# Involution network on one core: the end of the last image, with means taken two rows at a time, a transform over pairs of rows, sums on ScalarE and stores on SyncE

## The chip, the cores and the metric

The kernel runs on one NeuronCore of a Trainium2 chip. The metric is the device time of one execution in microseconds (us); a time without a profile is the median of several executions. Engines are named as in the profile: PE is TensorE (matmul), PEld its weight loads, DVE is VectorE, ACT is ScalarE, POOL is GpSimd and SP is SyncE, which here only issues DMAs. Everything is float32. An fp32 matmul shows in the profile as two passes, each with its own weight load and its own MATMUL record, so "x112" on a matmul line is 56 matmuls.

## The reference

The input is 4 images of 256 channels, 56 x 56. Four residual layers follow one another: `x = x + L(gn(x))` with a group norm over 32 groups of 8 channels ahead of each. Layers 0 and 2 are involutions (a 7 x 7 filter made per pixel and group from the image itself), layer 1 is a pair of 3 x 3 convolutions. Layer 3, whose end is changed here, is a pair of gates:

```python
def _L3_conv_ref(x, W, b):
    cf = jnp.fft.fft2(x, axes=(-2, -1)).real.mean(axis=(-2, -1))
    cf = jax.nn.sigmoid(cf @ W.T + b)
    x_cft = x * cf[:, :, None, None]
    sf = jnp.fft.fft2(x.mean(axis=1, keepdims=True), axes=(-2, -1)).real.mean(axis=1)
    x_sft = x * sf[:, None, :, :]
    return x_cft + x_sft
...
x = x + _L3_conv_ref(_gn(x), L3_conv_W, L3_conv_b)
```

The mean of the real part of a transform is its first pixel, so the channel gate `cf` needs only the normed value at pixel (0, 0) of every channel. The pixel gate `sf` is the real part of the 2-D transform of the mean over channels of the normed image. The output is `x + xn * (cf + sf)` with `xn = gn(x)`.

## The kernel before

The channels are two blocks `cb` of 128, one per set of partitions. Layers 0 and 2 share `involution_layer`. A unit is one image and one block; the last of the eight is image 3, block 1. In a unit, `tap_matrices` (L460) makes the filter matrices in 32 steps, with hooks: small pieces of other work, generators stepped by `place`, are put behind step n. DVE adds the bias in three steps of four (L489) and ACT in the fourth (L482). Then `apply` (L501) runs over seven columns `tx` of 8 pixels: PE multiplies (L513), ACT and DVE combine the four or two groups (L528, L533) and DVE adds into the image block `xs` (L540). `next_windows` (L371) transposes the strip of a later column on PE and has SP copy it about with four DMAs (L388, L390). `column_sums` (L924) takes the statistics of a finished column on DVE, one column late. Everything between `since` and `in_order` is pinned: each engine runs its instructions in the order in which the code emits them, and SP and POOL issue their DMAs in that order too.

The gates of images 0 to 2 are computed while later units run: `gate_chunk` (L668) works on POOL, which also issues their loads and stores. For image 3, block 0's channel mean goes through `channel_mean` (L568) as a hook, and block 1 comes after the last `apply`, in this order:

- `last_sums` takes the statistics of the last column; `last_normed(b, 0)` (L701) makes `xn` of block 0 on ACT (L715).
- `last_mean` (L724): the channel mean of block 1 before the group norm is known. One matmul for each column x of the image, with the 56 pixels of the column as weights (a stride of 56 elements) and the 16 group sums as the moving operand (L735), gives 56 rows x 56 columns x 16 groups in two PSUM banks.
- `norm_steps` (L190): statistics, two matmuls with `gavg` (L197, L208), DVE steps between them, and `rsqrt` with its power on POOL (L139).
- The mean goes on: L738 and L741 spread scale and shift, DVE multiplies 56 x 896 values (L747), sums over groups (L754) and adds (L757).
- `gate_factors` (L611): the channel gate (L623 on PE, a sigmoid on ACT at L630) and the first half of the transform over both blocks (L639, L649).
- `last_gates` (L760): the second half (L772), a product that lays eight rows side by side (L774), and then seven chunks `j` of 8 rows. In each, PE spreads `sf` over the partitions (L783), DVE forms `(sf + f) * xn` for each block (L787), block 0 is summed and stored by POOL (L789, L790), block 1 is finished by ACT, which has the original `x` folded in by a scale and a shift (L792), and stored by SP (L793).

`dead` gives space in a block that is no longer used, `one_bank` and `two_banks` give the next of four double PSUM banks. After the last instruction every engine drains and meets the others at a barrier (L1558 in the profile).

Of the kernel before, what the change touches and what calls it, by code (L numbers as in the profile page):

```python
# [10 lines left out]
F32 = mybir.dt.float32  # L11
AF = mybir.ActivationFunctionType
ALU = mybir.AluOpType
# [3 lines left out]
P = 128  # L17
B, C, H, W = 4, 256, 56, 56
NB = C // P
# [3 lines left out]
R = 64  # L23
# [3 lines left out]
CR = 8  # L27
# [9 lines left out]
NTY, NTX = -(-H // TY), W // TX  # L37
# [34 lines left out]
def net_kernel(  # L72
# [169 lines left out]
    def involution_layer(layer, xin, xout, red, span, sb, xs_of, ahead=None, pending=None):  # L242

        with ExitStack() as es:
# [315 lines left out]
            def dead(b, cb, at, n):  # L560

                if b < B - 1:
                    return xs_of[b, cb][:, at : at + n]
                if None not in xs_of:
                    xs_of[None] = new_block()
                return xs_of[None][:, at : at + n]
# [125 lines left out]
            last_xn = {}  # L692
# [8 lines left out]
            def last_normed(b, cb):  # L701
# [11 lines left out]
                for j, xn in enumerate(pieces):  # L713
# [7 lines left out]
                    )  # L721
                    yield

            def last_mean(b, bank):  # L724


                cb, ng = NB - 1, P // 8
                xs = xs_of[b, cb].rearrange("p (h w) -> p w h", w=W)
                rstd, shift = (t[:, cb : cb + 1] for t in norms[3][b])
                by = gavg_sb.rearrange("p (g i) -> p i g", i=8)[:, 0, :]  # L730
                m = W // 2
                pair = two_banks()
                means = pair[:H, :, : m * ng].rearrange("y i (x g) -> y i x g", g=ng)
                for x in range(W):
                    nc.tensor.matmul(means[:, x // m, x % m, :], xs[:, x, :], by, start=True, stop=True)  # L735
                yield

                nc.tensor.matmul(bank[:H, 1 : 1 + ng], rstd.to_broadcast([P, H]), by, start=True, stop=True)  # L738
                scales = dead(b, cb, 4 * CR * W + NB * C, 32)[:H]
                yield  # L740
                nc.tensor.matmul(  # L741
                    bank[:H, 1 + ng : 2 + ng], shift.to_broadcast([P, H]), cmean[:, 0:1], start=True, stop=True
                )
                nc.vector.tensor_scalar(first_of[b][:, cb : cb + 1], xs[:, 0, 0:1], rstd, shift, ALU.mult, ALU.add)
                nc.vector.tensor_scalar_mul(scales[:, :ng], bank[:H, 1 : 1 + ng], 8.0 / C)
                parts = dead(b, cb, 2 * CR * W, 2 * CR * W)[:H].rearrange("y (i x g) -> y i x g", i=2, g=ng)
                nc.vector.tensor_tensor(  # L747
                    parts,
                    means,
                    scales[:, :ng].unsqueeze(1).unsqueeze(1).to_broadcast([H, 2, m, ng]),  # L750
                    ALU.mult,
                )
                nc.vector.tensor_copy(scales[:, ng : ng + 1], bank[:H, 1 + ng : 2 + ng])
                nc.vector.tensor_reduce(  # L754
                    m2_of[cb].rearrange("y (i x) -> y i x", i=2), parts, mybir.AxisListType.X, ALU.add
                )
                nc.vector.tensor_scalar_add(m2_of[cb], m2_of[cb], scales[:, ng : ng + 1])  # L757
                yield

            def last_gates(b):  # L760
                rstd, shift = norms[3][b]

                inv = small.tile([P, 1], F32, name="inv", bufs=1)
                nc.vector.reciprocal(inv, rstd[:, 1:2])
                cfx = small.tile([P, 1], F32, name="cfx", bufs=1)
                nc.vector.tensor_add(cfx, cf_of[b][:, 1:2], inv)
                back = small.tile([P, 1], F32, name="back", bufs=1)
                nc.vector.scalar_tensor_tensor(back, shift[:, 1:2], -1.0, inv, ALU.mult, ALU.mult)


                ps = one_bank()
                nc.tensor.matmul(ps[:H, :W], half, cs2_sb, start=True, stop=True)  # L772
                rows = dead(b, NB - 1, 0, CR * W)[:H]
                nc.vector.tensor_tensor(  # L774
                    rows.rearrange("y (r w) -> y r w", r=CR),
                    ps[:H, :W].unsqueeze(1).to_broadcast([H, CR, W]),
                    last_xn[0][:H].unsqueeze(2).to_broadcast([H, CR, W]),
                    ALU.mult,
                )
                for j in range(NCHUNK):  # L780
                    at = slice(j * CR * W, (j + 1) * CR * W)
                    sf = one_bank()[:, : CR * W]
                    nc.tensor.matmul(sf, last_xn[1][:H, j : j + 1].to_broadcast([H, P]), rows, start=True, stop=True)  # L783
                    for cb in range(NB):
                        xs, xn = xs_of[b, cb][:, at], last_xn[j, cb]
                        f = cfx if cb == 1 else cf_of[b][:, cb : cb + 1]
                        nc.vector.scalar_tensor_tensor(xn, sf, f, xn, ALU.add, ALU.mult)  # L787
                        if cb == 0:
                            nc.gpsimd.tensor_tensor(xs, xs, xn, ALU.add)  # L789
                            nc.gpsimd.dma_start(ov[b, cb][:, at], xs)  # L790
                        else:
                            nc.scalar.activation(xs, xn, AF.Identity, bias=back)  # L792
                            nc.sync.dma_start(ov[b, cb][:, at], xs)  # L793


            def step(g):
# [2 lines left out]
            def place(hooks, g, at):  # L799

                for n in at:
                    hooks.setdefault(n, []).append(step(g))
# [57 lines left out]
            for u, (b, cb) in enumerate(units):  # L860
                hooks = hooks0 if u == 0 else {}
                if prev is not None:
                    pb, pc, st, last_sums = prev
                    hooks.setdefault(1, []).append(last_column(last_sums))
                    place(hooks, norm_of(layer + 1, pb, pc, st), (2, 6, 7, 11, 12, 13))
                    if layer == 2 and u < 3:
                        g = norm_of(2, B - 1, u - 1, pending[1][u - 1])
                        place(hooks, g, (19, 20, 22, 23, 25, 26))
                    if layer == 2:
                        place(hooks, channel_mean(pb, pc), (13, 17))  # L870
                        if pc == 1:
                            place(hooks, gate_factors(pb), (17, 24, 27, 28, 30, 31))
                        elif pb == B - 1:
                            factors = gate_factors(pb)
                            place(hooks, factors, (20,))
                            hooks.setdefault(22, []).append(last_ones)
                    if layer == 2 and cb == 1 and b > 0:
                        for n in (16, 22, 28):
                            hooks.setdefault(n, []).extend((next_gate, next_load))
# [44 lines left out]
                def column_sums(tx, st=st, img=img):  # L924
                    nc.vector.bn_stats(st[:, tx, :], img[:, :, tx * TX : (tx + 1) * TX])  # L925
# [2 lines left out]
                    late[0].append(ahead)  # L928

                for tx in range(NTX):  # L930
                    for f in early[tx]:
                        f()
                    apply(b, cb, kt, tx, xws[u * NTX + tx])
                    next_windows()
                    next_strip()
                    if tx > 0:
                        column_sums(tx - 1)
                    for f in late[tx]:
                        f()
# [7 lines left out]
            if layer == 2:  # L947
                run(last_normed(b, 0))
                bank = one_bank()
                mean, norm = last_mean(b, bank), norm_steps(st, lambda: bank, 3, b, cb)  # L950
                next(mean)
                for _ in range(5):
                    next(norm)
                next(mean)
                next(norm)
                next(mean)
                normed = last_normed(b, cb)
                for _ in range(2):
                    next(normed)
                next(factors)  # L960
                run(normed)
                for _ in range(2):
                    next(factors)
                last_gates(b)
            in_order(since)

# [595 lines left out]
```

## Time and profile before

| | us |
|---|---|
| median of three executions | 1864.59 (1862.81 to 1867.78) |
| the profiled execution, its own time | 1861.41 |
| its span, first to last instruction | 1859.5 |
| PE busy | 1705.2 (92%) |
| DVE busy | 1430.2 (77%) |
| ACT busy | 751.4 (40%) |
| POOL busy | 432.0 (23%) |
| from the last matmul of `apply` (1814.7) to the end | 44.8 |

The profiled execution is one of the faster ones, 3.2 us under the median. Times inside it are counted from its first instruction. "Busy" is the union of an engine's records; "mean ns" is the length of one record, which for matmuls overlaps its neighbours. PEclk is the clock that was granted to PE as a share of the full one. A note in brackets says how long the engine had been idle ahead of a line and what released it.

### The profile page before, as it was taken

The page shows a single profiled execution, that of the slowest core. Times are in us where ns is not written, and L with a number is a line of the kernel's source. Part 1 is how long each engine was busy: PE and PEld are TensorE (multiplying, and loading weights), DVE is VectorE, ACT ScalarE, POOL GpSimd, SP SyncE. Part 2 cuts the span into 40 slices and gives each one's busy share as a digit, 9 for nine tenths or more (in the row PEclk, how much of TensorE's full clock was granted, in tenths as well). Part 3 has the DMA queues.
Part 4 walks back from the last instruction along what each step waited for, and adds up shares of the span by engine and source line. Part 5 has one row for each costly group of instructions (what it writes and reads, how often), then busy time and mean ns, then how long its engine had stood idle before and what let it go on. Part 6 is the DMA issues. An engine that isn't in the chain of part 4 may idle for free.

```text
span 1859.5 us, 55572 instructions
## 1 busy us (share of the span) xinstructions
PE 1705.2 (92%) x24028; PEld 1501.5 (81%) x24028; DVE 1430.2 (77%) x2824; ACT 751.4 (40%) x1662; POOL 432.0 (23%) x615
## 2 busy tenths in 40 slices
PE   5999999999859999999999999997989899898886
PEld 3888888888748988898899889985877887877874
DVE  5687778776668988998889888874777778778764
ACT  2445445454413222231232312113656556565543
POOL 2323433244210000000000000000000663672683
PEclk9999999999969999999999999998999999999985
DMA  3445544453543111120121111132433765763652
GB/s 100 150 147 178 154 121 138 156 154 106 159 129 101 41 62 61 61 68 25 61 71 58 51 48 33 54 122 63 154 129 127 207 209 174 201 213 118 196 164 75
DMA packets 65504, 215.67 MB, mean 116 GB/s; under 512 B 13487, under 2 KB 20444, under 8 KB 61420
## 3 DMA queue, kind: packets, MB, share of 16 engines
q1 hardware_dynamic: 44364, 141.60, 24.6%
q0 software_dynamic: 14848, 65.85, 10.9%
q10 hardware_dynamic: 6048, 4.68, 0.8%
q8 instruction: 189, 3.10, 0.7%
q14 instruction: 55, 0.45, 0.1%
HBM read 76.23 MB, written 49.15 MB: 67 GB/s over the span
## 4 chain that ended last, share of the span: by engine, by line
PE 67%; DVE 20%; DMA 4%; issue 3%; POOL 3%; ACT 2%; SPq 0%; DVEq 0%; POOLq 0%; ACTq 0%
PE mm L1336 20%; PE ps L513 15%; DVE kt L489 11%; PE mm L1254 10%; PE ps L471 8%; PE mm L1225 6%; PE ps L381 4%; DMA xw<-xw 2%; PE ps L433 2%; DVE un L533 2%; ACT hp L452 1%; DMA gx<-x 1%; PE ps L783 1%; DVE st L925 1%; DMA xs<-in_x_dram 1%
## 5 line engine op out<-in xcount | busy, mean ns | idle before, releaser
L513 PE MATMUL ps<-kt,xw 126*32 126x48 f32 (+1 forms) x12544 | 385.2, 236 | 57.0 <-DMA xw<-xw 19.2
L513 PEld LDWEIGHTS ps<-kt,xw 126*32 126x32 f32 (+1 forms) x12544 | 345.9, 122 | 102.6 <-issue 47.8
L471 PE MATMUL ps<-hp,z_sb 64*126 64x133 f32 x6144 | 387.2, 281 | 15.6 <-DVE kt L489 5.3
L471 PEld LDWEIGHTS ps<-hp,z_sb 64*126 64x126 f32 x6144 | 369.1, 188 | 30.4 <-DVE kt L489 6.6
L489 DVE TENSOR_TENSOR kt<-ps,zb_sb 126x798 f32<-126x798 f32 x384 | 357.8, 978 | 42.9 <-PE ps L471 42.4
L1336 PE MATMUL mm<-v,u_sb 128*128 128x280 f32 (+1 forms) x1728 | 383.2, 383 | 3.3 <-DVE v L1161 3.3
L1336 PEld LDWEIGHTS mm<-v,u_sb 128*128 128x128 f32 x1728 | 326.2, 189 | 57.4 <-DVE v L1161 3.6
L482 ACT ACTIVATE kt<-ps,zb_sb 126x133 f32<-126x133 f32 x768 | 224.0, 441 | 173.8 <-PE ps L471 173.8
L1254 PE MATMUL mm<-v,u_sb 128*128 128x252 f32 (+1 forms) x936 | 211.9, 387 | 12.6 <-DVE v L1145 12.6
L1254 PEld LDWEIGHTS mm<-v,u_sb 128*128 128x128 f32 x936 | 177.7, 191 | 43.1 <-issue 12.6
L533 DVE SCALAR_TENSOR_TENSOR un<-ps,par_sb,un 128x240 f32<-128x240 f32 x224 | 98.2, 456 | 101.9 <-ACT un L526 97.8
L533 DVE SCALAR_TENSOR_TENSOR un<-ps,s,un 128x240 f32<-128x240 f32 x224 | 102.4, 457 | 91.0 <-ACT un L528 86.7
L1373 POOL DMA_DIRECT2D x<-xs x24 | 13.1, 546 | 683.9 <-DVE xs L1372 538.6
L1321 ACT ACTIVATE res<-xs,shift,norm_sb 128x1120 f32<-128x1120 f32 (+1 forms) x24 | 30.2, 1259 | 234.8 <-DVE xs L1372 107.3
L538 POOL TENSOR_TENSOR xs<-un,xs 128x240 f32<-128x240 f32 x112 | 72.3, 665 | 223.0 <-DVE un L533 223.0
L382 ACT COPY xw<-ps 126x896 f32<-126x896 f32 x112 | 101.6, 907 | 50.1 <-PE ps L381 43.3
L381 PE MATMUL ps<-ident_sb,strip_sb 128*126 128x128 f32 x784 | 112.3, 284 | 1.4 <-DVE kt L489 0.8
L526 ACT ACTIVATE un<-ps,par_sb 128x240 f32<-128x240 f32 x112 | 50.1, 448 | 137.5 <-PE ps L513 134.9
L528 ACT ACTIVATE un<-ps,bn_t,s 128x240 f32<-128x240 f32 x112 | 60.1, 538 | 100.8 <-PE ps L513 94.6
L139 POOL TENSOR_TENSOR norm_sb<-norm_sb,mhalf 128x1 f32<-128x1 f32 x32 | 19.2, 602 | 351.0 <-DVE norm_sb L138 350.9
L1225 PE MATMUL mm<-xs,u_sb 128*128 128x126 f32 (+1 forms) x792 | 98.3, 277 | 1.3 <-DVE xs L1188 1.0
L1225 PEld LDWEIGHTS mm<-xs,u_sb 128*128 128x128 f32 x792 | 94.3, 191 | 2.7 <-issue 1.4
(224 smaller groups left out, 1962.3 us busy)
## 6 DMA issues: line engine op xcount, KB each, us to landing
xw<-xw SPq DMA_DIRECT2D x168, 252.0 KB
xw<-xw SPq DMA_DIRECT2D x224, 126.0 KB
xw<-xw POOLq DMA_DIRECT2D x56, 252.0 KB, 4.5
xs<-x SPq DMA_DIRECT2D x24, 560.0 KB
x<-xs POOLq DMA_DIRECT2D x8, 1568.0 KB, 8.1
xs<-x SPq DMA_DIRECT2D x8, 1568.0 KB
xs<-in_x_dram SPq DMA_DIRECT2D x6, 1568.0 KB
x<-xs SPq DMA_DIRECT2D x6, 1568.0 KB
```

What stands on the lines that cost most here:

```text
L381: nc.tensor.transpose(ps[:Q, k * P : (k + 1) * P], flat[:, k * Q : (k + 1) * Q], ident_sb)
L382: nc.scalar.copy(xw[:, :NSB, :], ps[:Q, : NSB * P].rearrange("q (n c) -> q n c", n=NSB))
L471: nc.tensor.matmul(ps[:Q, i, k * NT : (k + 1) * NT], z_sb[i * R : (i + 1) * R, cb * GB // 2 + gp, z0 : z0 + Q], hp[i * R : (i + 1) * R, py ...
L482: nc.scalar.activation(kt[:, g0 + i, pb, :, k], ps[:Q, i, k * NT : (k + 1) * NT], AF.Identity, bias=zb_sb[:, cb * GB + g0 + i, p0 + k : p0 ...
L489: nc.vector.tensor_tensor(kt[:, g0 : g0 + 2, pb], ps[:Q, :, : PB * NT].rearrange("q i (k t) -> q i t k", k=PB), zb_sb[:, cb * GB + g0 : cb ...
L513: nc.tensor.matmul(v[m * j : m * j + m, i, :, k * TP : (k + 1) * TP], xw[:, window(ty), m * j : m * j + m], kt[:, ng * j : ng * j + ng, :, ...
L528: nc.scalar.activation(part, o[0], AF.Identity, bias=bn["t4"][:, cb : cb + 1], scale=bn["s4"][ng][:, 0, cb : cb + 1])
L533: nc.vector.scalar_tensor_tensor(part, o[e], s, part, ALU.mult, ALU.add)
L538: nc.gpsimd.tensor_tensor(dst, u, dst, ALU.add)
L1225: nc.tensor.matmul(ps[:, co * m : (co + 1) * m], u[ci][:, co * P : (co + 1) * P], v2[:, e, : n // 2, ci * WT : (ci + 1) * WT], start=(ci = ...
L1254: nc.tensor.matmul(ps, u1_sb[:, ci, dy, k, co * P : (co + 1) * P], v[:, k, dy * NB + ci : (dy + n - 1) * NB + ci + 1 : NB, :], start=(j == 0),
L1336: nc.tensor.matmul(ps, u2_sb[:, ci, dy, k, co * P : (co + 1) * P], v[:, k, dy * NB + ci : (dy + n - 1) * NB + ci + 1 : NB, :], start=(j == 0),
```

## The change

The change touches only image 3 of layer 2's run.

- `last_dft` (new), a hook at step 21 of the last unit's `tap_matrices`: POOL clears a 128 x 224 table `along`; SP fills it with four DMAs and a second table `down` with one.
- `first_half` (new), hooks 28 and 29: block 0's half of the transform's first stage, two matmuls and two DVE copies, is done there.
- In the last column of the last unit, `column_sums` of the column before is emitted ahead of `apply` and not behind it.
- `last_mean`: 28 matmuls, each with two whole rows (112 pixels, next to one another) as weights, into one bank, and each a step of the generator. Sixteen 128 x 128 matmuls on the identity (`warm(16)`) come ahead of them, and the norm's steps are emitted between them. The products are 112 x 448 and the sums 112 x 28.
- `last_gates`: the transform of block 1 over pairs of rows: one matmul with `along` (224 columns), a DVE copy, then four matmuls with `down`, which are summed in PSUM with the matmul of block 0's half.
- Both blocks' outputs are finished by ACT as a scale and a shift, and all fourteen stores are issued by SP. POOL has no part in `last_gates`.

```diff
+            def last_dft(b):
+                n = 3 * CR * W
+                along = dead(b, NB - 1, n, 4 * W).rearrange("p (e c k) -> p e c k", e=2, c=2)
+                nc.gpsimd.memset(along, 0.0)
+                for e in range(2):
+                    for c in range(2):
+                        nc.sync.dma_start(along[e * W : (e + 1) * W, e, c], cs2[c * R : c * R + W])
+                down = dead(b, NB - 1, n + 4 * W, 4 * H).rearrange("p (e c k) -> p e c k", e=2, c=2)
+                nc.sync.dma_start(
+                    down[: H // 2], cs.rearrange("(y e) (c k) -> y e c k", e=2, c=2)
+                )
+                last_xn["dft"] = along, down
+            def first_half(b):
+                ps = one_bank()
+                for i in range(2):
+                    at = slice(i * R, i * R + W)
+                    nc.tensor.matmul(ps[at, :H], m2_of[0], sin_sb if i else cs2_sb[:H], start=True, stop=True)
+                yield
+                for i in range(2):
+                    at = slice(i * R, i * R + W)
+                    nc.vector.tensor_copy(half[at], ps[at, :H])
+                yield
...
-                for x in range(W):
-                    nc.tensor.matmul(means[:, x // m, x % m, :], xs[:, x, :], by, start=True, stop=True)
-                yield
+                for k in range(H // 2):
+                    nc.tensor.matmul(means[:, k, :], xs[:, k * n : (k + 1) * n], by, start=True, stop=True)
+                    yield
...
             def last_gates(b):
+                along, down = last_xn["dft"]
+                rows = dead(b, NB - 1, 0, CR * W)
+                ps = one_bank()
+                nc.tensor.matmul(
+                    ps[: H // 2, : 4 * W],
+                    last_xn["mean"],
+                    along[: 2 * W].rearrange("p e c k -> p (e c k)"),
+                    start=True,
+                    stop=True,
                 )
+                part = rows[: H // 2, : 4 * W].rearrange("p (e c k) -> p e c k", e=2, c=2)
+                nc.vector.tensor_copy(rows[: H // 2, : 4 * W], ps[: H // 2, : 4 * W])
+                ps = one_bank()
+                nc.tensor.matmul(ps[:H, :W], half, cs2_sb, start=True, stop=False)
+                for i in range(4):
+                    e, c = divmod(i, 2)
+                    nc.tensor.matmul(
+                        ps[:H, :W], down[: H // 2, e, c], part[:, e, c], start=False, stop=(i == 3)
+                    )
...
-                        f = cfx if cb == 1 else cf_of[b][:, cb : cb + 1]
-                        nc.vector.scalar_tensor_tensor(xn, sf, f, xn, ALU.add, ALU.mult)
-                        if cb == 0:
-                            nc.gpsimd.tensor_tensor(xs, xs, xn, ALU.add)
-                            nc.gpsimd.dma_start(ov[b, cb][:, at], xs)
-                        else:
-                            nc.scalar.activation(xs, xn, AF.Identity, bias=back)
-                            nc.sync.dma_start(ov[b, cb][:, at], xs)
+                        nc.vector.scalar_tensor_tensor(xn, sf, cfx[:, cb : cb + 1], xn, ALU.add, ALU.mult)
+                        nc.scalar.activation(xs, xn, AF.Identity, bias=back[:, cb : cb + 1])
+                        nc.sync.dma_start(ov[b, cb][:, at], xs)
...
+                            hooks.setdefault(21, []).append(lambda pb=pb: last_dft(pb))
                             hooks.setdefault(22, []).append(last_ones)
+                            place(hooks, first_half(pb), (28, 29))
...
+                    if layer == 2 and u == len(units) - 1 and tx == NTX - 1:
+                        column_sums(tx - 1)
...
-                    if tx > 0:
+                    if tx > 0 and not (layer == 2 and u == len(units) - 1 and tx == NTX - 1):
                         column_sums(tx - 1)
...
-                next(mean)
-                for _ in range(5):
-                    next(norm)
+                warm(16)
+                for _ in range(2):
+                    for _ in range(7):
+                        next(mean)
+                    for _ in range(2):
+                        next(norm)
+                for _ in range(H // 2 - 14):
+                    next(mean)
+                next(norm)
                 next(mean)
                 next(norm)
                 next(mean)
...
-                for _ in range(2):
-                    next(factors)
                 last_gates(b)
```

More of the change, by code (lines that the diff above doesn't have):

```diff
@@ L724, in last_mean @@
+            def first_half(b):
[8 more added lines that the diff above has]
+                yield
             def last_mean(b, bank):
-                cb, ng = NB - 1, P // 8
@@ L728, in last_mean @@
-                xs = xs_of[b, cb].rearrange("p (h w) -> p w h", w=W)
+                cb, ng, n = NB - 1, P // 8, 2 * W
+                xs = xs_of[b, cb]
                 rstd, shift = (t[:, cb : cb + 1] for t in norms[3][b])
                 by = gavg_sb.rearrange("p (g i) -> p i g", i=8)[:, 0, :]
-                m = W // 2
-                pair = two_banks()
-                means = pair[:H, :, : m * ng].rearrange("y i (x g) -> y i x g", g=ng)
-                for x in range(W):
-                    nc.tensor.matmul(means[:, x // m, x % m, :], xs[:, x, :], by, start=True, stop=True)
@@ L736, in last_mean @@
-                yield
-                nc.tensor.matmul(bank[:H, 1 : 1 + ng], rstd.to_broadcast([P, H]), by, start=True, stop=True)
-                scales = dead(b, cb, 4 * CR * W + NB * C, 32)[:H]
+                ps = one_bank()
+                means = ps[:n, : H // 2 * ng].rearrange("p (k g) -> p k g", g=ng)
+                for k in range(H // 2):
+                    nc.tensor.matmul(means[:, k, :], xs[:, k * n : (k + 1) * n], by, start=True, stop=True)
+                    yield
+                nc.tensor.matmul(bank[:n, 1 : 1 + ng], rstd.to_broadcast([P, n]), by, start=True, stop=True)
@@ L740, in last_mean @@
+                scales = dead(b, cb, 4 * CR * W + NB * C, 64)[:n]
                 yield
                 nc.tensor.matmul(
-                    bank[:H, 1 + ng : 2 + ng], shift.to_broadcast([P, H]), cmean[:, 0:1], start=True, stop=True
+                    bank[:n, 1 + ng : 2 + ng], shift.to_broadcast([P, n]), cmean[:, 0:1], start=True, stop=True
                 )
-                nc.vector.tensor_scalar(first_of[b][:, cb : cb + 1], xs[:, 0, 0:1], rstd, shift, ALU.mult, ALU.add)
-                nc.vector.tensor_scalar_mul(scales[:, :ng], bank[:H, 1 : 1 + ng], 8.0 / C)
@@ L746, in last_mean @@
-                parts = dead(b, cb, 2 * CR * W, 2 * CR * W)[:H].rearrange("y (i x g) -> y i x g", i=2, g=ng)
+                nc.vector.tensor_scalar(first_of[b][:, cb : cb + 1], xs[:, 0:1], rstd, shift, ALU.mult, ALU.add)
+                nc.vector.tensor_scalar_mul(scales[:, :ng], bank[:n, 1 : 1 + ng], 8.0 / C)
+                parts = dead(b, cb, 2 * CR * W, CR * W)[:n].rearrange("p (k g) -> p k g", g=ng)
                 nc.vector.tensor_tensor(
[L748 to L751, printed above, removed]
-                )
@@ L753, in last_mean @@
[L753 to L757, printed above, removed]
+                    parts, means, scales[:, :ng].unsqueeze(1).to_broadcast([n, H // 2, ng]), ALU.mult
+                )
+                nc.vector.tensor_copy(scales[:, ng : ng + 1], bank[:n, 1 + ng : 2 + ng])
@@ L758, in last_mean @@
+                m = last_xn["mean"] = scales[:, 32 : 32 + H // 2]
+                nc.vector.tensor_reduce(m, parts, mybir.AxisListType.X, ALU.add)
+                nc.vector.tensor_scalar_add(m, m, scales[:, ng : ng + 1])
                 yield
             def last_gates(b):
-                rstd, shift = norms[3][b]
-                inv = small.tile([P, 1], F32, name="inv", bufs=1)
-                nc.vector.reciprocal(inv, rstd[:, 1:2])
-                cfx = small.tile([P, 1], F32, name="cfx", bufs=1)
@@ L766, in last_gates @@
[L766 to L773, printed above, removed]
+                along, down = last_xn["dft"]
+                rows = dead(b, NB - 1, 0, CR * W)
@@ new lines, in last_gates @@
+                ps = one_bank()
[8 more added lines that the diff above has]
+                nc.vector.tensor_copy(rows[: H // 2, : 4 * W], ps[: H // 2, : 4 * W])
+                ps = one_bank()
@@ new lines, in last_gates @@
+                nc.tensor.matmul(ps[:H, :W], half, cs2_sb, start=True, stop=False)
[3 more added lines that the diff above has]
+                        ps[:H, :W], down[: H // 2, e, c], part[:, e, c], start=False, stop=(i == 3)
+                    )
+                rstd, shift = norms[3][b]
+                inv, cfx, back = (small.tile([P, NB], F32, name=f"last{i}", bufs=1) for i in range(3))
+                nc.vector.reciprocal(inv, rstd)
@@ L774, in last_gates @@
+                nc.vector.tensor_add(cfx, cf_of[b], inv)
+                rows = dead(b, NB - 1, 2 * CR * W, CR * W)[:H]
                 nc.vector.tensor_tensor(
@@ L779, in last_gates @@
                 )
+                nc.vector.scalar_tensor_tensor(back, shift, -1.0, inv, ALU.mult, ALU.mult)
                 for j in range(NCHUNK):
```

## Prediction

> **What bounds the kernel now.** I read the share of busy time first, but the change lives in the last 45 us, so I went on to the timeline of each engine there, the windows with the granted clock, and the records of the barrier. PE after the last `apply`, by its timeline:
>
> ```profile
> 1814.70 11.75 PE L735 MATMUL ps<-gavg_sb,xs 128*56 128x16 f32 x112
> ...
> 1826.38 0.59 PE L197 MATMUL ps<-mv,gavg_sb 128*128 128x1 f32 x2
> ...
> 1829.29 0.37 PE L738 MATMUL ps<-gavg_sb,norm_sb 128*56 128x16 f32 x2 [0.90 <-POOL norm_sb L139]
> ...
> 1835.26 10.79 PE L783 MATMUL ps<-xs 56*128 56x448 f32 x14 [1.06 <-ACT xs L715]
> ```
>
> The stretch is four stages in a row: means (11.7), norm (2.9, PE waiting for DVE and POOL), gates (6.0), chunks. In the chunks PE gives one per 1.49 us (two passes of 0.745); DVE needs 2 x 0.60 and idles 0.22, ACT works 0.67 of each 1.49. Only POOL is slower: its sum of 1.14 and store of 0.56 come 2.03 us apart, so it finishes 4 us behind the others. What follows is in the records of the barrier (least, median and longest ns, then first and last start) and of SP's waits:
>
> ```profile
> 1850.07 1.14 POOL L789 TENSOR_TENSOR xs<-xs,hp 128x448 f32<-128x448 f32 x1
> 1851.50 0.56 POOL L790 DMA_DIRECT2D out_dram<-xs  x1 [0.30 <-POOL xs L789]
> ...
> L1558 POOLq DRAIN  x3: 40/102/7271, 1851.5 to 1859.3; - x3
> L1558 SPq DRAIN  x3: 7/7/7, 1854.3 to 1859.0; - x3
> ...
> L1558 ACTq DRAIN  x2: 14/356/697, 1847.4 to 1859.0; - x2
> ...
> SPq L1558 <- DMA out_dram<-xs: 5.3, 1, 5.3
> SPq L1558 <- PEq L1558: 5.0, 2, 4.6
> ```
>
> POOL's drain starts at 1851.50 with its last store and lasts 7.27 us, to 1858.77. ACT's drain ends with its last work (1848.1). SP sees the last store land at 1853.7, is ready at 1854.4 and then waits 4.6 us: put down to PE, but PE's drain was over at 1846.1, and the only one not done is POOL. So the end is POOL's last store plus its drain, plus 0.75 of barrier.
>
> The clock of PE, by windows of time (busy PE, PEld, DVE, ACT, POOL, then PEclk, DMA share, GB/s):
>
> ```profile
> 1438.47:1441.88 3.41, 2.27 (x26) 2.08 (x24) 2.77 (x8) 2.02 (x4) 0.00 (x0) 1.00 0.00 0
> 1441.88:1445.30 3.42, 3.42 (x33) 3.42 (x34) 0.56 (x3) 2.01 (x7) 0.55 (x1) 0.50 0.73 224
> ...
> 1776.38:1779.80 3.42, 2.29 (x38) 1.98 (x36) 2.84 (x4) 1.75 (x6) 3.04 (x4) 1.00 0.29 83
> ...
> 1814.70:1817.00 2.30, 2.30 (x30) 2.30 (x23) 2.20 (x6) 2.16 (x4) 0.59 (x1) 1.00 0.29 107
> 1817.00:1820.00 3.00, 3.00 (x32) 3.00 (x31) 2.13 (x5) 2.93 (x5) 0.00 (x0) 0.56 0.00 0
> ...
> 1841.00:1846.00 5.00, 5.00 (x7) 1.67 (x5) 4.21 (x7) 2.11 (x4) 4.07 (x6) 0.50 0.71 262
> ```
>
> [...] L735, all loads, loses the clock at 1817.34 with PE 100% busy. From there all runs at half clock; the chunks' matmuls (56 rows of 128) don't win it back.
>
> **The change part by part.**
>
> *Ahead of the end.* At step 28 DVE runs L489 back to back (1772.9 to 1779.2) and PE waits for it, so `first_half`'s two copies (L649, 0.214 each) delay all behind: 0.45, between 0 (hidden in PE's later waits for window DMAs) and 0.9 (its matmuls and bank too). `last_dft` is a memset on POOL (nearest L293, 0.23 for 161 columns) and five issues on SP (L608, 0.35 for a small one): 2 us. SP is idle from 1773 to 1784.5 and POOL ends 13 us before it is needed: nothing, if cover holds. The statistics moved ahead of the last `apply` push DVE's additions back 0.6, to 1818.35, and end when they did.
>
> *Means.* Count from T0 = 1814.70; the norm is done and L738 starts at T0 + 14.6. After: `warm(16)` is 32 passes at 0.124 (L1225, 128 x 126: 98.3 us by 792), 4.0, which covers the wait for `xs` (T0 + 3.65). Then 56 passes with 112 weights and 4 of the norm with 128. Contiguous loads of 128 with one column: L623 took 1.14 for 8 at full clock (1707.7) and 1.86 at half (1829.8); without the last record's own length, 0.127 and 0.215 a pass, so 0.111 and 0.188 for 112. L735's 0.105 for 56 strided weights is the same at either clock. All at full clock: T0 + 10.8; all at half: T0 + 15.5. [...] Then 27 passes are fast and 33 take 6.3: T0 + 13.3. I take that, a gain of 1.3; the norm runs inside (its DVE and POOL steps need 0.8 and 1.5, behind seven and fourteen matmuls).
>
> *Gates.* Before: 5.97 from L738 to L783. After, at half clock: scale spread and multiplied 0.8; products 448 instead of 896, 0.65 (L774, 0.616 for 448 from PSUM, against L747's 1.08); copy 0.15; sums 0.61; add 0.2: mean at 2.45, 0.8 sooner. But PE spends 0.4 more on the wider spreading, and L623's second half needs the bank that the copy reads, to 2.55. `along`: 2 passes of 224 at 0.374, and 0.37 to DVE's start, as ahead of L787: 3.7. Copy 0.38 (between L649 and L774): 4.1. Eight passes at 0.11 and 0.5 to DVE (L772 to L774): 5.5. L774: 6.1, L783 at 6.2 to 6.5. I take a loss of 0.4. ACT's last `xn` ends about then, but only the last chunk reads it.
>
> *Chunks and end.* PE still gives a chunk per 1.49. ACT has 2 x 0.67, SP 2 x 0.33 of issue. Stores ask 448 KB per 1.49 us, 300 GB/s; a window at 1422 moved 452. [...] Two more DVE operations of 0.6 a chunk would make 2.4 against 1.49, 6.4 us over seven chunks, a total gain of 1.6; ACT has the room[...]. Last ACT still ends where it did (1848.06). From there to the end: before 11.4. After: SP's issue, landing 2.4 (POOL's stores: 2.2 to 3.1; SP's own not shown, the small L663 was waited on for 1.6), SP's ten semaphores 0.7, barrier 0.75, in all 3.9. POOL's last work is the power at about T0 + 9, so even a full 7.3 drain ends before 1835. Gain 7.5, bounds 6.8 to 8.3.
>
> *Sum:* -0.45 + 1.3 - 0.4 + 7.5 = 8.0. Against the profiled execution (span 1859.5, 1.9 around it, 1861.4): 1853.4. It stands 3.2 under the median of 1864.59, to which I carry the difference: **1856.6**.
>
> **Rivals.**
> 1. *Clock holds through the means*[...]: M at T0 + 10.8, 2.5 better, 1854.1. For: 112 of 128 columns loaded, where L735 had 56. [...] 0.13.
> 2. *The drain isn't POOL's own*: it ends with all stores' retiring, and 5.8 us after the last landing remain. Then POOL's removal gives only the earlier landing (1850.5 for 1853.7, 3.2) and with the other terms' 0.45 it is 3.7 in all: 1860.9. For: nothing shows what the drain does. Against: the store had landed at 1853.7, and ACT's and DVE's drains end with their work. 0.10.
> 3. *Slower: SP held by the memset.* SP's four tables' DMAs wait for POOL, and behind them on SP are the windows, first issued at 1784.47, with PE already short of one at 1790.5. Each us past that is paid in full: at 1792.5 the gain is gone, and past 1798 the kernel is over 0.3% slower. Held to 1800: 1872. POOL would reach the memset, between its gates at 1763.6 and 1768.9, over 20 us late; its longest wait for a load nearby is 2.0. 0.04.
> 4. *The change doesn't do what it says*: [...] the means all run at half clock, T0 + 15.5: 2.2 worse, 1858.8. Inside the likeliest case's own range.
>
> **The numbers.** Likeliest (0.73): 1856.6, own range 1854.5 to 1859. 0.3% is 5.6 us, about what a measurement of this kernel can tell from no change; faster by that is below 1859.0. Likeliest 0.71, first rival 0.13, a fifth of the second 0.02: 0.86 faster. 0.09 within (most of the second, edges), 0.05 slower (third, a little unseen). The range of 8 in 10 reaches from 1853[...] to 1861 (second).
>
> **What would show it.** POOL's drain starts before 1830 and SP's is last, with the barrier within 4.5 us of the last ACT; if the end still lies 10 us behind it, the second rival holds. The means take 32 passes at 0.124, then 56 at 0.111 turning to 0.188 at one moment; a full clock up to L738 is the first rival. L738 to L783 near 6.4. First windows of the last unit on SP issued within 0.5 us of 1784.5, else the third. Wrong altogether if ACT or SP, not PE, paces the chunks: then they are over 1.49 us apart.

## The result, and the profile after

| | before | after |
|---|---|---|
| median, us | 1867.31 (7 executions, 1862.81 to 1871.63) | 1858.43 (7 executions, 1853.13 to 1863.00) |
| ratio of the times, 95% interval | | 0.9955 (0.9936 to 0.9974) |
| the profiled execution, its own time | 1861.41 | 1863.00 |
| its span | 1859.5 | 1860.8 |
| start of the last matmul of `apply`, T0 | 1814.6 | 1828.5 |
| T0 to the end | 44.9 | 32.3 |

T0 is read here as the start of the last matmul of `apply`; the prediction counts from the start of the matmul behind it, 0.1 later. The changed kernel is faster by 8.4 us in the ratio, and its profiled execution is nevertheless the slowest of its seven, with a longer span than the one shown of before. These two spans can't be compared as they stand. The profiled execution of after comes to the first matmul of `apply` 2.3 us late (73.9 for 71.6, L513), to the last unit's last product for its filters 13.9 us late (1791.5 for 1777.6, L471), and most of that lag is there before the first of the new hooks: 11.2 us at the last product with the reducing weights (1689.4 for 1678.1, L433), about 100 us ahead of them. Over the twelve profiled executions told of here T0 lies between 1809.0 and 1828.5, and the two that run the old code ahead of T0 have 1814.6 and 1826.2. So I count every stage from T0, as the prediction did, and there the kernel after is 12.6 us shorter in these two executions.

Its PE by the timeline, after the last `apply`:

```profile
1828.61 3.84 PE L261 MATMUL ps<-ident_sb 128*128 128x128 f32 x32
1832.29 1.46 PE L760 MATMUL ps<-gavg_sb,xs 128*112 128x16 f32 x14
1833.60 0.36 PE L197 MATMUL ps<-mv,gavg_sb 128*128 128x1 f32 x2
...
1835.42 3.64 PE L760 MATMUL ps<-gavg_sb,xs 128*112 128x16 f32 x28
1838.89 0.53 PE L763 MATMUL ps<-gavg_sb,norm_sb 128*112 128x16 f32 x2
...
1844.91 10.79 PE L819 MATMUL ps<-xs 56*128 56x448 f32 x14 [0.80 <-DVE last L815]
```

From start to start, the warm-up's 32 passes take 3.68, 0.115 each, and the first fourteen of the means 1.31, 0.094 each. The last 28 take 3.47, a mixture of 0.094 and slower ones. The spread of the norm's scale (L763, before L738) starts at T0 + 10.4 for T0 + 14.6, the chunks (L819, before L783) 6.0 behind it for 5.97, and the chunks' fourteen passes last 10.79, as before. The clock in these stages (busy PE, PEld, DVE, ACT, POOL, then PEclk, DMA share, GB/s):

```profile
1832.45:1835.45 3.00, 3.00 (x34) 3.00 (x32) 0.64 (x4) 1.39 (x3) 0.00 (x0) 1.00 0.00 0
1835.45:1837.40 1.95, 1.95 (x22) 1.95 (x22) 0.59 (x3) 0.76 (x2) 0.57 (x1) 0.99 0.00 0
1837.40:1838.90 1.50, 1.50 (x11) 1.50 (x10) 0.00 (x0) 0.65 (x1) 0.00 (x0) 0.50 0.00 0
1838.90:1844.90 6.00, 4.86 (x25) 3.77 (x26) 2.99 (x10) 3.64 (x7) 0.00 (x0) 0.50 0.00 1
```

PE is 100% busy in the first three rows, and the clock falls between the second and the third, at 1837.4, 4.9 us behind the end of the warm-up. The end, by POOL's and ACT's last records in the timeline, the records of the barrier (L1597, before L1558; least, median and longest ns, first and last start) and SP's waits:

```profile
1835.85 0.57 POOL L139 TENSOR_TENSOR norm_sb<-norm_sb,mhalf 128x1 f32<-128x1 f32 x1 [7.86 <-DVE norm_sb L138]
1857.04 0.67 ACT L823 ACTIVATE xs<-xs,last 128x448 f32<-128x448 f32 x1
...
L1597 POOLq DRAIN  x3: 40/102/6749, 1835.8 to 1860.5; - x3
L1597 SPq DRAIN  x3: 7/7/7, 1860.0 to 1860.3; - x3
...
L1597 ACTq DRAIN  x2: 14/356/699, 1857.0 to 1860.3; - x2
...
SPq L1597 <- DMA out_dram<-xs: 1.3, 2, 0.8
SPq L1597 <- PEq L1597: 0.7, 2, 0.5
```

POOL's long drain starts with its last instruction, the power at 1835.85, and ends at 1842.6, fifteen us before ACT has done. SP's wait for others at the barrier is 0.5, where it was 4.6. The span ends 3.09 us after ACT's last sum; before it was 11.44.

### The profile page after: what moved, and what is told of

It reads as the page before. It is cut to its first block, busy times and chain, and to the rows that moved or that the text cites. A ratio compares the mean times of both kernels' runs of the same rounds, so it can differ in the third digit from the quotient of the medians.

```text
span 1860.8 us, 55545 instructions
## 1 busy us (share of the span) xinstructions
PE 1715.2 (92%) x24010; PEld 1509.3 (81%) x24010; DVE 1429.6 (77%) x2825; ACT 755.8 (41%) x1669; POOL 419.8 (23%) x602
## 4 chain that ended last, share of the span: by engine, by line
PE 67%; DVE 22%; DMA 4%; issue 3%; ACT 2%; POOL 1%; SPq 1%; ACTq 0%; POOLq 0%; DVEq 0%
PE mm L1375 19%; PE ps L513 15%; DVE kt L489 12%; PE mm L1293 10%; PE ps L471 8%; PE mm L1264 6%; PE ps L381 4%; DMA xw<-xw 3%; PE ps L433 2%; DVE un L533 2%; ACT hp L452 1%; PE ps L596 1%; DVE res L1368 1%; PE ps L819 1%; POOL norm_sb L139 1%
## 5 line engine op out<-in xcount | busy, mean ns | idle before, releaser
L513 PE MATMUL ps<-kt,xw 126*32 126x48 f32 (+1 forms) x12544 | 385.5, 237 | 57.5 <-issue 21.6
L513 PEld LDWEIGHTS ps<-kt,xw 126*32 126x32 f32 (+1 forms) x12544 | 346.4, 123 | 103.1 <-issue 50.7
L471 PE MATMUL ps<-hp,z_sb 64*126 64x133 f32 x6144 | 394.2, 284 | 16.0 <-DVE kt L489 5.3
L471 PEld LDWEIGHTS ps<-hp,z_sb 64*126 64x126 f32 x6144 | 375.2, 191 | 31.1 <-DVE kt L489 6.6
L489 DVE TENSOR_TENSOR kt<-ps,zb_sb 126x798 f32<-126x798 f32 x384 | 358.2, 979 | 49.6 <-PE ps L471 49.0
L1293 PE MATMUL mm<-v,u_sb 128*128 128x252 f32 (+1 forms) x936 | 211.0, 386 | 12.6 <-DVE v L1184 12.6
L1293 PEld LDWEIGHTS mm<-v,u_sb 128*128 128x128 f32 x936 | 177.1, 190 | 42.9 <-issue 12.6
```

The source lines that it names most:

```text
L471: nc.tensor.matmul(ps[:Q, i, k * NT : (k + 1) * NT], z_sb[i * R : (i + 1) * R, cb * GB // 2 + gp, z0 : z0 + Q], hp[i * R : (i + 1) * R, py ...
L489: nc.vector.tensor_tensor(kt[:, g0 : g0 + 2, pb], ps[:Q, :, : PB * NT].rearrange("q i (k t) -> q i t k", k=PB), zb_sb[:, cb * GB + g0 : cb ...
L513: nc.tensor.matmul(v[m * j : m * j + m, i, :, k * TP : (k + 1) * TP], xw[:, window(ty), m * j : m * j + m], kt[:, ng * j : ng * j + ng, :, ...
L1293: nc.tensor.matmul(ps, u1_sb[:, ci, dy, k, co * P : (co + 1) * P], v[:, k, dy * NB + ci : (dy + n - 1) * NB + ci + 1 : NB, :], start=(j == 0),
```

## The experiments

Stages in every profiled execution: M is the start of the spread matmul behind the means, S the start of the chunks, "fall" the moment at which the granted clock went from 1.00 to 0.50, counted from the end of the warm-up, or of `apply` where there is none.

| kernel | T0 to M | fall | M to S | S to the end | T0 to the end |
|---|---|---|---|---|---|
| before | 14.7 | 2.6 | 6.0 | 24.2 | 44.9 |
| before, stores by SP | 14.7 | 2.8 | 6.0 | 19.7 | 40.4 |
| after | 10.4 | 4.9 | 6.0 | 15.9 | 32.3 |
| after, again | 9.9 | 5.5 | 6.0 | 15.9 | 31.8 |
| after, POOL last | 12.1 | 3.1 | 6.0 | 20.2 | 38.3 |
| after, no warm-up | 12.0 | 2.9 | 6.0 | 15.9 | 33.9 |
| after, warm-up of ten | 11.0 | 4.0 | 6.0 | 15.9 | 32.9 |
| after, norm behind the means | 12.2 | 5.2 | 6.0 | 15.9 | 34.2 |
| after, transform's half late | 10.8 | 4.6 | 6.1 | 15.8 | 32.7 |
| after, sums on DVE | 12.5 | 2.6 | 6.0 | 22.6 | 41.1 |
| after, 128-row chunks | 10.8 | 4.6 | 6.0 | 15.1 | 31.9 |
| ten and 128 rows together | 11.3 | 2.5 | 6.0 | 15.1 | 32.4 |

The variants ran once each, except the changed kernel and the last row, and T0 alone differs by up to 19.5 us between executions; so of these only the stages are compared, not the times. M and S are read to 0.1. The theory: the gain is POOL's absence from the end plus the shorter means, and nothing else. The rivals: the drain belongs to the stores and not to POOL; the means are shorter for another reason than the passes and the clock; the early parts cost what the end gives.

**The kernel before, with block 0's stores on SP.** One line; POOL still makes the sums.

```diff
-                            nc.gpsimd.dma_start(ov[b, cb][:, at], xs)
+                            nc.sync.dma_start(ov[b, cb][:, at], xs)
```

> The kernel before, with block 0's seven stores issued by SP (L790 on SP's queue) and POOL still making block 0's sums. Theory (POOL's drain of 6.2 to 6.7 us follows its last instruction, whatever that is): POOL's sums come without the 0.56 of issue, so its last sum ends some 1.5 us after ACT's last instruction where it ended 3.1 us after it, but its drain follows all the same: the end lies about 9 us after ACT's last instruction (11.4 before). Rival (the drain belongs to POOL's own stores): the last store lands 2.0 to 2.4 us after it is issued and the end lies about 5 us after ACT's last instruction.

POOL's last records, its drain and SP's wait:

```profile
1857.34 2.33 POOL L789 TENSOR_TENSOR xs<-xs,hp 128x448 f32<-128x448 f32 x2 [0.65 <-DVE hp L787]
...
L1558 POOLq DRAIN  x3: 40/102/7289, 1858.5 to 1866.3; - x3
...
SPq L1558 <- PEq L1558: 4.1, 2, 3.6
```

Measured from the last ACT to the end: 6.90, between the two expectations. I had placed POOL's last sum 1.5 us behind ACT; without its store to issue POOL keeps pace with the chunks and ends its last sum at 1859.67, with ACT's (1859.70). The drain ends at 1865.8, 6.1 us behind that sum, and the span 0.8 later. So the issue of stores had cost POOL its lag (4.5 us of the end), and the drain costs 3.8 more as long as POOL works to the end.

**The change, with one POOL instruction behind ACT's last sum.** It stores nothing.

```diff
                         nc.sync.dma_start(ov[b, cb][:, at], xs)
+                nc.gpsimd.memset(last_xn[NCHUNK - 1, NB - 1][:, :1], 0.0)
```

> The changed kernel with one memset of a single column on POOL that has to wait for ACT's last activation. Theory (the drain of 6.2 to 6.7 us follows POOL's last instruction of any kind): the drain starts with the memset and ends about 6.5 us after ACT's last instruction, and the end of the span lies 7.3 us after ACT's last instruction, 4.2 more than the 3.1 of the changed kernel. Rival (a long drain needs a POOL store shortly ahead of it): the end stays 3.1 to 3.3 us after ACT's last instruction.

POOL's only record at the end, its drain and SP's wait:

```profile
1849.26 0.10 POOL L825 MEMSET xs<- 128x1 f32 x1 [23.00 <-ACT xs L823]
...
L1598 POOLq DRAIN  x3: 40/102/6251, 1849.2 to 1856.0; - x3
...
SPq L1598 <- PEq L1598: 5.0, 2, 4.2
```

A memset of one column, 0.10 us long, puts the end 7.4 us behind ACT for 3.09. SP had seen its stores land by 1851.4. From the end of POOL's last instruction to the end of its drain are 6.1 us here (1849.36 to 1855.49), 6.1 behind the last sum in the run above, 6.1 behind the power in the changed kernel (1836.42 to 1842.55; the drain itself takes 6.75 there, as it does in the runs with the sums on DVE and with both edits), and 6.7 behind the last store's issue in the kernel before. Between these kinds of instruction the figure differs by 0.6 at most, and the landing of stores does not enter: here none is POOL's. The second rival of the prediction falls, in the changed kernel's own profile too: there the span ends 1.1 us after SP has seen the last store land (1859.7), where that rival would have had 5.8.

**No warm-up, and one of ten.**

```diff
-                warm(16)
+                warm(10)        # and in the other run: no line
```

> The changed kernel without the sixteen warm-up matmuls. Theory ([...]the warm-up mostly fills the wait for xs): the means start when xs is whole, about 2.4 us after the last matmul of apply[...]; L763 starts 11.5 to 13.5 us after apply's end (10.3 in the changed kernel's profile[...]). Rival (without the warm-up the clock is lost at once, all passes at 0.19): about 14 us. Rival two (the warm-up is 3.8 us of pure delay): about 8.7 us.

> The changed kernel with ten warm-up matmuls instead of sixteen, 2.4 us instead of 3.8, which is about the wait for xs. Theory: [...] L763 comes 1.4 us sooner[...]. Rival (sixteen are needed to hold the clock through the means): the fall comes within 1 us of the warm-up's end[...], and L763 over 13 us after apply's end.

PE by the timeline, first without the warm-up:

```profile
1822.32 1.52 PE L760 MATMUL ps<-gavg_sb,xs 128*112 128x16 f32 x14 [1.29 <-ACT hp L715]
...
1824.54 2.77 PE L760 MATMUL ps<-gavg_sb,xs 128*112 128x16 f32 x14
...
1827.58 5.39 PE L760 MATMUL ps<-gavg_sb,xs 128*112 128x16 f32 x28
```

and with ten:

```profile
1809.17 2.50 PE L261 MATMUL ps<-ident_sb 128*128 128x128 f32 x20
1811.57 1.52 PE L760 MATMUL ps<-gavg_sb,xs 128*112 128x16 f32 x14
...
1815.18 4.96 PE L760 MATMUL ps<-gavg_sb,xs 128*112 128x16 f32 x28
```

Without the warm-up the means start at T0 + 1.5 and the clock falls at T0 + 3.1, so that the last 28 passes take 5.22 to the start of the next line (1832.80), 0.186 each; M comes at T0 + 12.0. So without any warm-up the passes of two rows, with the norm between them, bring M 2.7 us sooner than in the kernel before, in this one execution. The first rows of the image are there at T0 + 1.5, not at T0 + 3.65 as I had it for the whole block: the warm-up's length is paid, not covered. Sixteen had the clock fall at T0 + 7.1 in the run with POOL last, later by about the warm-up's length: at a like fall (2.9 and 3.1 in the table) none has M at T0 + 12.0 and sixteen at 12.1, so a gain from the warm-up is not shown. Ten gave T0 + 11.0. Sixteen gave 9.9 to 12.5 in six executions, by where the fall came. At a like fall (2.5 to 2.6) ten has 11.3, in the combined run below, and sixteen 12.5: most of the 1.4 us (12 passes at 0.115) of the six matmuls left out. Which length is best on the mean, these runs don't show.

**The norm's steps behind the means, not between them.**

```diff
-                for _ in range(2):
-                    for _ in range(7):
-                        next(mean)
-                    for _ in range(2):
-                        next(norm)
-                for _ in range(H // 2 - 14):
-                    next(mean)
-                next(norm)
+                for _ in range(H // 2):
+                    next(mean)
+                for _ in range(5):
+                    next(norm)
```

> The changed kernel with the norm's two matmuls and its power emitted behind all 28 means instead of between them. Theory: the norm's chain (2.9 us in the kernel before, from the last mean to L738) is uncovered again: L763 starts 2.4 to 2.9 us later against the last mean than it does in the changed kernel, where it follows it at once. Rival (the chain is short at full clock): 1.5 us or less.

```profile
1821.95 5.67 PE L760 MATMUL ps<-gavg_sb,xs 128*112 128x16 f32 x56
1827.47 0.57 PE L197 MATMUL ps<-mv,gavg_sb 128*128 128x1 f32 x2
1828.87 0.58 PE L208 MATMUL ps<-d,gavg_sb 128*128 128x1 f32 x2 [0.84 <-DVE d L205]
1830.36 0.55 PE L763 MATMUL ps<-gavg_sb,norm_sb 128*112 128x16 f32 x2 [0.91 <-POOL norm_sb L139]
```

This run had the clock nearly through (56 passes in 5.67), and its M is still at T0 + 12.2. L763 starts 2.9 us after L197, the very figure of the kernel before (2.9), with PE idle 0.84 and 0.91 for DVE and POOL. In the changed kernel L763 follows the last mean. Against the two executions with a fall as late (9.9 and 10.4) the interleaving is worth 1.8 to 2.3, about half of the 4.3 by which M came sooner in the profiled execution. The rest is the passes of two rows less the warm-up; no run has the old passes, one column each, in the new order, so their own share is a remainder and not measured.

**The transform's first half in the tail again.** It runs behind `last_normed`, ahead of `last_gates`.

```diff
-                            place(hooks, first_half(pb), (28, 29))
...
                 run(normed)
+                run(first_half(b))
                 last_gates(b)
```

> The changed kernel with block 0's half of the transform's first stage taken back from the hooks into the end, just ahead of the last gates. Theory: the last unit up to apply's end is 0.45 us shorter (49.9 us from the first L593 of that unit to apply's end in the changed kernel, 49.3 before), and the end is longer by what PE (four passes, 0.2 us) and DVE (two copies, 0.43) cannot hide: L763 to L819 takes 6.3 to 6.7 us instead of 6.0. Net within 0.3 us of the changed kernel. Rival (the copies are hidden by PE's work in the end): 6.0 still, a net gain of 0.5.

DVE by the timeline: the copies fit ahead of one for which DVE would have waited.

```profile
1826.00 0.24 DVE L778 TENSOR_SCALAR xs<-xs 112x28 f32<-112x28 f32 x1
1826.56 0.44 DVE L747 COPY half<-ps 56x56 f32<-56x56 f32 x2 [0.32 <-PE ps L743]
1827.42 0.38 DVE L794 COPY xs<-ps 28x224 f32<-28x224 f32 x1 [0.42 <-PE ps L786]
```

M to S is 6.1 for 6.0. What the copies cost at hook 28 isn't seen either: from the first matmul of block 0's channel mean in the last unit (L593) to T0 are 49.2 and 49.6 us in the two runs with the old code, 47.9 here, and 48.0 to 50.5, 49.3 on the mean, in the nine with the copies there.

**The sums on DVE.** DVE multiplies by `cf` without `1/rstd`, and an addition on DVE takes the place of ACT's scale and shift.

```diff
-                        nc.vector.scalar_tensor_tensor(xn, sf, cfx[:, cb : cb + 1], xn, ALU.add, ALU.mult)
-                        nc.scalar.activation(xs, xn, AF.Identity, bias=back[:, cb : cb + 1])
+                        nc.vector.scalar_tensor_tensor(xn, sf, cf_of[b][:, cb : cb + 1], xn, ALU.add, ALU.mult)
+                        nc.vector.tensor_tensor(xs, xs, xn, ALU.add)
```

> The changed kernel with all final sums on DVE (a product and a sum per block and chunk) and none on ACT[...]. Theory (DVE becomes the pace of the chunks): four operations of 0.60 to 0.68 a chunk, 2.4 to 2.6 us apart instead of 1.49, so that from L819's start to the end it takes 22 us instead of 15.9. Rival[...]: 1.8 a chunk, 18 us.

Nine us windows of the chunks (columns as above):

```profile
1837.00:1846.00 9.00, 9.00 (x13) 3.54 (x11) 8.45 (x14) 0.00 (x0) 0.00 (x0) 0.50 0.36 136
1846.00:1855.00 9.00, 0.23 (x1) 0.00 (x0) 8.72 (x15) 0.00 (x0) 0.00 (x0) 0.50 0.51 188
```

DVE is full and PE has long finished; a chunk takes 2.51, and S to the end 22.6 for 15.9. This placement would have cost 6.7 us here; I had 6.4. DVE's sum is hardly shorter than ACT's (0.62 for 0.67), and DVE is the engine that has no room.

**Chunks spread from 128 rows.** The 56 rows of `sf` stand in a block whose other 72 rows are zero, so the matmul has 128 rows for the same product. At the clock of 0.50 its first three chunks come 1.49 apart (DVE's products at 1836.27, 1837.76 and 1839.25), as with 56 rows. Whether the clock comes back with 128 is the question. The first line of the edit clears the block, in `last_dft`.

```diff
+                nc.gpsimd.memset(dead(b, NB - 1, 4 * CR * W + NB * C + 64, CR * W), 0.0)
...
-                rows = dead(b, NB - 1, 2 * CR * W, CR * W)[:H]
+                full = dead(b, NB - 1, 4 * CR * W + NB * C + 64, CR * W)
+                rows = full[:H]
...
-                    nc.tensor.matmul(sf, last_xn[1][:H, j : j + 1].to_broadcast([H, P]), rows, start=True, stop=True)
+                    nc.tensor.matmul(sf, last_xn[1][:, j : j + 1].to_broadcast([P, P]), full, start=True, stop=True)
```

> The changed kernel with the chunks' matmuls on 128 rows instead of 56 (the added rows hold zeros in both operands, the result is the same; the 128-row operand lies in its own cleared space). Theory[...]: the clock comes back[...], and from there a chunk takes ACT's 1.34 us instead of 1.49: the stage from L819's start to the end is 0.3 to 0.6 us shorter than 15.9. Rival (the rows don't matter): the clock stays at half, passes stay 0.745 us apart, 15.9.

Windows of the chunks:

```profile
1834.40:1836.40 2.00, 2.00 (x3) 1.14 (x4) 0.14 (x1) 0.13 (x1) 0.00 (x0) 0.50 0.00 0
1836.40:1839.80 3.40, 3.40 (x6) 1.39 (x5) 2.96 (x5) 2.58 (x4) 0.00 (x0) 0.50 0.35 130
1839.80:1845.00 5.20, 2.79 (x8) 1.14 (x6) 5.20 (x10) 5.03 (x9) 0.00 (x0) 1.00 0.93 343
```

The clock goes from 0.50 to 1.00 5.4 us after the chunks begin; with 56 rows PE was as busy for 10.8 us and it stayed at 0.50. From there DVE and ACT pace (sums 0.59 apart, a chunk per 1.19) and the stores fill the DMA engines to 0.93. The last ACT comes 1.2 sooner behind S than in the changed kernel, 0.4 of which is lost again behind it (3.5 from there to the end for 3.1); the stage is 0.8 shorter, a little more than expected.

**The changed kernel again, and ten with 128 rows together.**

> The changed kernel once more, unchanged, timed in five rounds beside the kernel before and beside the combined version. Every term found so far lies behind T0 (the last matmul of apply), where the two profiled executions differ by 12.6 us. If that is all that the change does, the ratio is 0.993 to 0.996, that is 8 to 13 us, and the stage from T0 to the end is 32 to 34.5 us again. A rival: the five table DMAs, the early half of the transform and the statistics moved ahead of the last apply cost 3 to 5 us ahead of T0, which the spread of T0 between executions (1809 to 1828) hides in single profiles; then the ratio stays at 0.995 to 0.9965 although the stage is over 12 us shorter.

> The changed kernel with two edits together that were each looked at alone: ten warm-up matmuls for sixteen, and chunks spread from 128 rows (72 of them zeros) for 56. If both terms add: 1.4 us off the means where they still run mostly at full clock, 0.8 off the chunks; T0 to the end 30 to 32.5 us against 32 to 34.5, ratio to the kernel before about 0.001 under that of the changed kernel in the same job. The rival: the shorter warm-up lets the clock fall that much earlier[...], and the means' last part then runs at 0.188 a pass for 0.104; then the start of the spread stays at T0 + 11 to 12 and only the 0.8 of the chunks is left, which five rounds can hardly show.

| | median, us | ratio to the kernel before, 95% interval |
|---|---|---|
| before, 14 executions | 1869.23 (1861.34 to 1877.84) | |
| after, 8 | 1855.08 (1852.71 to 1860.62) | 0.9932 (0.9904 to 0.9961) |
| both edits, 7 | 1852.28 (1849.92 to 1861.14) | 0.9920 (0.9889 to 0.9951) |

The combined version keeps the chunks' 0.8 (15.1). Its means met an early fall and start the spread at T0 + 11.3, so the shorter warm-up shows no gain in that profile. Its median is the lowest, 2.8 under the changed kernel's, but the intervals overlap nearly whole: that it beats the changed kernel is not shown. The changed kernel's stage from T0 is again 31.8.

## Why the prediction was right, point by point

The forecast was 1856.6, 8.0 under the kernel before; the medians are 1858.43 and, in the second comparison, 1855.08, and the ratios stand for 8.4 and 12.7 us. The direction and the main term, the end, held by their mechanism. That the first comparison comes so close to 8.0 is in part chance: my terms behind T0 were together some 4 us too small, all to the careful side, and the first comparison happens to show less than the stages do.

- **Ahead of the end, -0.45.** Not to be seen: the scatter of that stretch (47.9 to 50.5) is larger. The cover of the table loads held. SP issued them from 1786.39 to 1789.7, 3.3 us where I had 2, and its first window at 1798.26; less the 13.9 us by which that execution was late, this is 1784.4, and I had 1784.5. The third rival (SP held by the memset) did not come about.
- **Means, gain 1.3.** It was 4.3 and 4.8 in the two profiles of the changed kernel, and 3.7 on the mean over the six executions that have these means unchanged (M at T0 + 11.1; the prediction's 13.3 is 13.4 from this T0). The mechanism was right: passes of two rows, full clock (1.00) to one moment and half (0.50) from there. Three terms of the sum were mis-sized. The warm-up takes 3.68, not 4.0. A fast pass with 112 weights takes 0.094, not 0.111 (slow ones 0.186, as I had them): the 3.0 us that I gave to fast passes hold 32 and not 27, and five slow passes fewer are 0.9. And the fall comes 4.4 us after the warm-up on the mean over the seven executions with sixteen (2.6 to 5.5), not 3.0, which was my estimate; what sets the moment was not shown. In each us of delay 10.6 passes go at 0.094 that would have taken 2.0, so the 1.4 are worth 1.4. The three are 2.6 of sooner start, for the 2.4 by which I was off.
- **The first rival, a clock that holds through the means.** Its T0 + 10.8 is near the mean of 11.1, but the clock did not hold: in the changed kernel's profile PE was 100% busy all through and the clock went from 1.00 to 0.50 at 1837.4, 1.5 ahead of M, and it fell ahead of M in all twelve. With the passes as they measured, a full clock up to M would have been T0 + 9.5 (3.8, 56 times 0.094 and 4 of the norm at 0.11); the two executions with the latest fall came near that, at 9.9 and 10.4. So the first rival did not occur, though its time nearly did; that is chance.
- **Gates, loss 0.4.** None: 6.0 in all. The term that was too large is the copy of the transform's first product, the eight passes behind it and the wait for them: from the copy of `along`'s product to DVE's product 1.46 (1842.68 to 1844.14), where I had 1.8 (3.7 to 5.5); the steps ahead of them took 3.79 for 3.7.
- **Chunks.** 1.49 as before, S to the last ACT's end 12.80 in both. ACT kept up with both sums, and the run with the sums on DVE shows that those would cost 6.7 us at this place.
- **End, gain 7.5.** 8.35. The drain was the mechanism, as argued. Of my 3.9 from the last ACT, 3.09 were needed: the issue is 0.38, the barrier behind SP's drain 0.8, and 1.9 lie between, in which the landing and SP's semaphores run beside each other, where I had taken 2.4 for the landing and then 0.7 for the semaphores.

From T0 the sum is 12.6 in the profiled execution: 4.3 means, 0 gates, 8.3 end, where my own was 8.4 (1.3, -0.4, 7.5). On the mean of the six executions the means give 3.7, and the sum is 12.0. Eleven to thirteen us over 1867 are a ratio of 0.994 to 0.993. The first comparison has that at the edge of its interval (4.9 to 12.0 us), the second in the middle (7.3 to 17.9). Whether something ahead of T0 gives part of it back, a few us at most, stays open: no run separates it from the scatter of T0. What scatters there was not tried, nor what the drain does in its 6.1 us.

## What to carry to other kernels

See which engine's drain is last at the closing barrier: here a POOL that works to the end puts its 6.1 us behind its last instruction, be it 0.1 us long, so its work at the end is better given to an engine with room. Where a chain of small steps on other engines stands beside a run of independent matmuls, interleave them in the order of issue (1.8 to 2.3 us here). And compare single profiles by stages counted from a common mark: 12.6 us of gain were invisible in the two spans.

## What the runs showed of the hardware that was not expected

- The clock fell from 1.00 to 0.50 between 2.5 and 5.5 us after the end of the warm-up, or of `apply` where there was none, a spread of 3.0 over the twelve profiled executions; in the seven with sixteen warm-up matmuls it came after 2.6 to 5.5. In the us around the fall PE was 100% busy in the changed kernel (1836.90 to 1837.90) and 72% without the warm-up (1823.45 to 1824.45).
- With 128 rows, 72 of them zeros, the clock went from 0.50 to 1.00 5.4 us after the chunks began (4.9 in the combined run); with 56 rows it stayed at 0.50 for the chunks' 10.8 us with PE 100% busy.
- POOL's drain ends 6.1 us after the end of a memset, a sum or a power, and 6.7 after a store's issue; ACT's (0.70, from the start of its last sum) ends with the work.
